# A graph layer on one core: first loads, left-over products, tap transforms and the last gate moved

## Chip, core and metric

The kernel runs on one core of a Trainium2 chip, as one launch. The metric is the device time of that launch in microseconds (us); for several runs it is their median. All data is 32-bit floating point.

In the text PE is TensorE (matrix products), DVE is VectorE, ACT is ScalarE, POOL is GpSimd, and SP is the engine that does nothing but issue transfers. ACT and POOL issue transfers too. An engine works through its own instructions strictly in order.

## What is computed

For 32 graphs (batches) of 512 nodes with 256 channels, with x the input and adj the adjacency matrix:

```python
h = jnp.maximum(_layernorm(x, axis=-1), 0.0)
xc = jnp.transpose(h, (0, 2, 1))
c = relu(_bn(_conv1d(xc, conv1_w, 0), ...))          # 1 tap
c = _bn(_conv1d(c, conv2_w, 8), ...)                 # 17 taps along the nodes
x_conv = jnp.transpose(relu(c + xc), (0, 2, 1))
s = h @ w_se.T + b_se                                # 3 features per node
A = jnp.exp(-dist(s, s)) * adj
x_nmp = einsum('bnm,bmd->bnd', A, relu(h @ w_msg.T + b_msg))
gi = concat([x_conv, x_nmp]) @ w_ih.T + b_ih
gh = h @ w_hh.T + b_hh                               # gates r, z, n of 256 each
r, z = sigmoid(gi_r + gh_r), sigmoid(gi_z + gh_z)
n = tanh(gi_n + r * gh_n)
out = x + (1 - z) * n + z * h
```

## The kernel before, in words

The 17-tap convolution is done in the frequency domain. The nodes of a batch are cut into 8 windows of 64, so that 16 batches fill the 128 partitions; these 16 batches are a *group*, and there are two groups (batches 0 to 15, 16 to 31). A *unit* is one of 40 frequency units of a group: `product` (L368) multiplies the windows' spectra (tile `xf`) with the unit's weights (tile `wt`, two loads of 256 KB from DRAM by `load_unit`, L344), with three complex products. `prepare` (L357) gets for it, on POOL, the sum of the weights (`wsum`, L351) and two combinations of the spectra (`both`, L364 and L365). There are three `wt` buffers, two of `wsum` and two of `both`, so unit u can be loaded when unit u-3 has been used, and prepared when unit u-2 has.

**Stages.** (1) `first_part(0)`, L776: for each batch `statistics` (L279, BNStats and BNStatsAggregate on DVE, a power on POOL), `normalise` (L292, DVE), `transpose_h` (L301, PE transposes, DVE takes the maximum with 0 into `hT`, SP stores it), `conv1` (L311, PE; DVE adds the shift, ACT the relu) and `windows_to_freq` (L326, PE; ACT copies to `xf`). Between these, `weights_to_freq` (L248) turns 64 slices of the tap weights `w2p` into frequency weights. (2) `nodes(0)`, L880: for each batch the messages (`message`, L423), node features (`features`, L438), their distances (`factors`, `affinity`), and `aggregate` (L476); the products of units 0 to 36 are spread over its 16 rounds. (3) `first_part(1)` with the three products that are left over, 37 to 39, given as the lists `left`, of which `fill()` runs one at each of its calls (L800). (4) `nodes(1)` with the 40 products of group two. (5) The late stage: for 16 pairs of batches the inverse transform (`inverse`), and the gates (`gates_rz`, `gate_n`), each as seven products of combined blocks Q1 to Q7. For the last pair the gates r and n come first, and `last_z` (L637) computes z last and the output with it.

**Order.** The two first parts and the late stage stand under `manual_schedule`: each engine gets its instructions in the order of the program text. In the two node loops a scheduling layer orders them. Transfers that one engine issues go out in its order. They signal their end on a few shared counters, and the built program lets an issue wait until the earlier transfer on the same counter has landed; in the profile this is a wait of SP for a transfer that has nothing to do with its own data.

**The places of the change.**
- Start: `first_part(0)` runs the first two steps of `weights_to_freq` ahead of `conv1(0)` (L811 to L817). They need the first slices of `w2p`, which SP loads at L243.
- Group two: x of batches 16 to 18 is loaded by POOL after the node loop (L931); statistics, normalise and the first transposes of batch 16 follow. `left` holds four lists; product 37 comes ahead of the transposes of batch 16, 38 and 39 come after `conv1(16)`.
- End: in `last_z`, the block Q3 (L677) is added in two halves into the bank that held Q5 (`b3`), so it waits until Q5's sum has been read. `blended` (L641) does everything for one quarter in a row: add the other terms (L644), sigmoid on ACT (L647), multiply (L648), transpose 32 by 32 (L652), add to x (L654); `store` (L769) issues four transfers by turns on SP and ACT. `early_out` (L742) writes the n part (transposes L761, add L750); ahead of it `h - n` is computed at L735.

Of the kernel before, what the change touches and what calls it, by code (L numbers as in the profile page):

```python
# [11 lines left out]
FP = mybir.dt.float32  # L12
AF = mybir.ActivationFunctionType
ALU = mybir.AluOpType

P = 128
# [49 lines left out]
def gnn_layer(  # L66
# [38 lines left out]
    def bank(name):  # L105
        return psum.tile([P, N], FP, tag="bank", name=name)
# [7 lines left out]
            queue.dma_start(dst[32 * g : 32 * (g + 1)], src[64 * g : 64 * (g + 1)].rearrange("(e i) o -> i e o", e=DC))  # L114

    def load_x(b, queue=nc.sync):
        X[b] = pools["first"].tile([P, NC, D], FP, tag="x", name=f"x_{b}", bufs=3)
        queue.dma_start(X[b], x[b].rearrange("(c p) d -> p c d", p=P))


# [79 lines left out]
    def shift_w1():  # L200
        nc.scalar.copy(shift1_row.rearrange("p (i q) -> p i q", i=DC), by_parity(row1[1][:, :D]))
# [435 lines left out]
    def last_z(p, terms):  # L637

        d, o, ks = RZ[p], 1, range(K3)

        def blended(src, other, i, j, t=slice(0, N)):  # L641
            z, dst = d[:, DC + i, j, t], d[:, i, j, t]
            if other is not None:
                nc.vector.tensor_add(z, other[:, t], src[:, t])  # L644
                src = z
            g = DC + i
            nc.scalar.activation(z, src, AF.Sigmoid, bias=brz[:, g : g + 1], scale=1.0)  # L647
            nc.vector.tensor_mul(dst, dst, z)  # L648
            js, half = slice(t.start // 32, t.stop // 32), slice(32 * i, 32 * (i + 1))
            if (p, j) not in OUT:  # L650
                OUT[p, j] = pools["late"].tile([P, N // 32, D // 4], FP, tag="o", name=f"o_{p}_{j}", bufs=2)
            nc.vector.transpose(OUT[p, j][:, js, half], dst.rearrange("p (j k) -> p j k", k=32))  # L652
            x = XP[p][j][:, js, half]
            nc.vector.tensor_add(x, x, OUT[p, j][:, js, half])  # L654

        b1, b2, b3, b4 = (bank(f"pz{k}_{p}") for k in range(1, 5))
        into(b1, Q1, o, ks, terms, True)
        p1 = temp("p1", f"z{p}")
        nc.scalar.copy(p1, b1)
        into(b2, Q6, o, ks, terms, True)  # L660
        u2 = temp("u2", f"z{p}")
        nc.vector.tensor_add(u2, p1, b2)
        into(b1, Q2, o, ks, terms, False)
        blended(b1, None, 0, 0)
        early_out(p, 1, 1)
        into(b2, Q7, o, ks, terms, False)
        u3 = temp("u3", f"z{p}")
        nc.vector.tensor_add(u3, p1, b2)
        early_out(p, 0, 1)
        into(b4, Q4, o, ks, terms, True)  # L670
        blended(b4, u3, 1, 0)
        store(p, 0, [nc.sync, nc.scalar])
        into(b3, Q5, o, ks, terms, True)
        blended(b3, u3, 1, 1)
        for h in range(2):
            t = slice(h * N // 2, (h + 1) * N // 2)
            into(b3, Q3, o, ks, terms, False, t)  # L677
            blended(b3, u2, 0, 1, t)
            store(p, 1, [nc.sync, nc.scalar], t)

    def gate_n(p, terms, last):
        rz, o = RZ[p], 2
        NT[p] = nt = pools["late"].tile([P, DC, 2, N], FP, tag="nt", name=f"nt_{p}", bufs=2)
        h, i_ = [0], [1, 2]
        add, mul = ALU.add, ALU.mult

        def pair(q, banks, first):
            for bk, ks in zip(banks, (h, i_)):
                into(bk, q, o, ks, terms, first)

        def scaled(bk, other, other_i, i, j):

            n = nt[:, i, j, :]
            if other is None:
                nc.vector.scalar_tensor_tensor(n, bk, b_hn[:, i : i + 1], rz[:, i, j, :], op0=add, op1=mul)
            else:
                nc.vector.scalar_tensor_tensor(n, bk, b_hn[:, i : i + 1], other, op0=add, op1=add)
                nc.vector.tensor_mul(n, n, rz[:, i, j, :])
                nc.vector.tensor_add(n, n, other_i)

        def closing(bk, i, j):
            n = nt[:, i, j, :]
            nc.vector.tensor_add(n, n, bk)  # L703
            nc.scalar.activation(n, n, AF.Tanh, bias=b_in[:, i : i + 1], scale=1.0)  # L704

        x1 = [bank(f"pn1_{p}_{k}") for k in range(2)]
        pair(Q1, x1, True)
        p1 = [temp("p1", f"n{p}_{k}") for k in range(2)]
        for k in range(2):
            nc.scalar.copy(p1[k], x1[k])  # L710
        x2 = [bank(f"pn2_{p}_{k}") for k in range(2)]
        pair(Q6, x2, True)
        u2 = [temp("u2", f"n{p}_{k}") for k in range(2)]
        for k in range(2):
            nc.vector.tensor_add(u2[k], p1[k], x2[k])
        pair(Q2, x1, False)
        scaled(x1[0], None, None, 0, 0)
        closing(x1[1], 0, 0)
        pair(Q7, x2, False)
        u3 = [temp("u3", f"n{p}_{k}") for k in range(2)]  # L720
        for k in range(2):
            nc.vector.tensor_add(u3[k], p1[k], x2[k])
        x3 = [bank(f"pn3_{p}_{k}") for k in range(2)]
        pair(Q5, x3, True)
        scaled(x3[0], u3[0], u3[1], 1, 1)
        closing(x3[1], 1, 1)
        pair(Q4, x2, False)
        scaled(x2[0], p1[0], p1[1], 1, 0)
        closing(x2[1], 1, 0)
        pair(Q3, x3, False)  # L730
        scaled(x3[0], u2[0], u2[1], 0, 1)
        closing(x3[1], 0, 1)
        for i, j in ((0, 0), (1, 1), (1, 0), (0, 1)):

            nc.vector.tensor_sub(rz[:, i, j, :], HP[p][:, 2 * i + j, :], nt[:, i, j, :])  # L735
            if last and j == 0:
                early_out(p, i, j)
            elif not last:

                blend(p, i, j, nc.gpsimd if p == B // 2 - 2 and i != j else nc.vector)  # L740


    def early_out(p, i, j):
        if (i, j) == (0, 0):
            OUT[p] = pools["work"].tile([P, N // 32, D // 4], FP, tag="x", name=f"on_{p}", bufs=3)
        OUT[p, j] = OUT[p]
        to_tokens(p, j, i)
        o = OUT.pop((p, j))
        if i != j:
            nc.vector.tensor_add(XP[p][j], XP[p][j], o)  # L750

    def blend(p, i, j, engine):
        n, d = NT[p][:, i, j, :], RZ[p][:, i, j, :]
# [25 lines left out]
    def first_part(g, freq, between, left=()):  # L779
# [1 line left out]

        b0, b1 = g * GB, (g + 1) * GB
        for b in range(b0, b0 + 3):
            if b not in X:
                load_x(b)
        if g == 0:
            t = XN[b0] = pools["first"].tile([P, NC, D], FP, tag="xn", name="rows", bufs=2)
# [2 lines left out]
            batch_norm("bn1", scale1, shift1, nc.gpsimd)  # L790
            bn1_row(0, scale1, ones, diags)
            bn1_row(1, shift1, ones, diags)
        statistics(b0)
        normalise(b0)
        if g == 0:
            scale_w1()
            shift_w1()
        left = list(left)

        def fill():  # L800
# [1 line left out]
                step()  # L802

        fill()
        statistics(b0 + 1)
        transpose_h(b0)
        normalise(b0 + 1)
        fill()
        for b in range(b0, b1):
            if b + 3 < b1:  # L810
                load_x(b + 3, nc.gpsimd)  # L811
            if b == b0:
                if g == 0:
                    for steps in between(0):
                        for step in steps:
                            step()
                conv1(b)  # L817
                fill()
            if b + 2 < b1:
                statistics(b + 2)  # L820
            if b + 1 < b1:
                transpose_h(b + 1)
            if b + 2 < b1:
                normalise(b + 2)
            if b == b0:
                fill()
                xf = freq(g)
            one, two = between(b - b0) if b > 0 else ([], [])
            if b > b0:
                conv1(b)  # L830
            if b == b1 - 1:
                load_h(b0)
            for step in one:
                step()
            if b > b0:
                windows_to_freq(b - 1, xf)
            for step in two:
                step()
# [13 lines left out]
    with tc.tile_pool(name="freq", bufs=1) as fpool:  # L852
# [22 lines left out]
                xf = first_part(0, freq_tile, between)  # L875


        LEFT = 3

        def nodes(g, xf, units, last):  # L880

# [32 lines left out]
                for u in mine[2:]:  # L914
                    product(pools["pw"], g, u, xf)

        with phase("pw"):
            with phase("nodes"):
                nodes(0, xf, range(UNITS - LEFT), GB)
            with phase("first", "sums"):  # L920
                combine = combine_weights()

# [5 lines left out]
                    two = [partial(sum_unit, pools["pw"], 1, b - GB + 3)] if b > GB - 3 else []  # L928
                    return combine[b - 2] if 1 < b < len(combine) + 2 else [], two

                for b in range(GB, GB + 3):  # L931
                    load_x(b, nc.gpsimd)

                pw, (u0, u1, u2) = pools["pw"], range(UNITS - LEFT, UNITS)
                left = [[partial(prepare, pw, 0, u1, xf), partial(product, pw, 0, u0, xf)],
                        [partial(prepare, pw, 0, u2, xf)],
                        [partial(product, pw, 0, u1, xf)],
                        [partial(product, pw, 0, u2, xf)]]
                prepare(pw, 0, u0, xf)
                load_unit(0, u1)  # L940
                load_unit(0, u2)
                with tc.manual_schedule():
                    xf = first_part(1, freq_tile, between, left)
            with phase("nodes"):
# [77 lines left out]
```

## Time and profile before

| what | value |
|---|---|
| median of 8 runs | 1866.17 us (1863.29 to 1872.11) |
| the profiled execution | 1870.86 us, of which 1869.1 us span |
| mean granted TensorE clock in it | 0.992 |
| PE busy | 1826.5 us |
| DVE, ACT, POOL busy | 1115.8, 578.2, 580.1 us |
| DMA | 289.25 MB, mean 155 GB/s |

The span goes from the first to the last recorded instruction or transfer; the time of the execution is 1.76 us more. Busy time is time in which an engine has an instruction under way. "Idle before <- releaser" is the time that an engine stood still ahead of an instruction, with what ended it. In a list of waits the numbers are us in total, times, and the longest. In a timeline a row gives the start, the length of a merged run of equal instructions, the engine (SPq, ACTq: issue of transfers), the line, and in brackets the idle time ahead of it. A matmul of 32-bit data shows as two records.

### The profile page before, as it was taken

The page shows a single profiled execution, that of the slowest core. Times are in us where ns is not written, and L with a number is a line of the kernel's source. Part 1 is how long each engine was busy: PE and PEld are TensorE (multiplying, and loading weights), DVE is VectorE, ACT ScalarE, POOL GpSimd, SP SyncE. Part 2 cuts the span into 40 slices and gives each one's busy share as a digit, 9 for nine tenths or more (in the row PEclk, how much of TensorE's full clock was granted, in tenths as well). Part 3 has the DMA queues.
Part 4 walks back from the last instruction along what each step waited for, and adds up shares of the span by engine and source line. Part 5 has one row for each costly group of instructions (what it writes and reads, how often), then busy time and mean ns, then how long its engine had stood idle before and what let it go on. Part 6 is the DMA issues. An engine that isn't in the chain of part 4 may idle for free.

```text
span 1869.1 us, 20076 instructions
## 1 busy us (share of the span) xinstructions
PE 1826.5 (98%) x6598; PEld 1087.7 (58%) x6598; DVE 1115.8 (60%) x2238; ACT 578.2 (31%) x1075; POOL 580.1 (31%) x563
## 2 busy tenths in 40 slices
PE   7999999999899999999999999999999999999997
PEld 5767566666698666666555544555455544555443
DVE  6875555554796554555165566645665466645666
ACT  3455434332145443333222212222122222222121
POOL 3331243344342344442613322132212323133220
PEclk9999999999999999999999999999999999999998
DMA  8998988866567998767513442244422442234412
GB/s 214 297 265 234 214 225 246 218 176 187 186 221 226 228 255 238 228 192 236 179 42 77 119 118 85 37 116 119 112 71 55 118 119 90 52 95 118 118 30 39
DMA packets 306299, 289.25 MB, mean 155 GB/s; under 512 B 148028, under 2 KB 235612, under 8 KB 305812
## 3 DMA queue, kind: packets, MB, share of 16 engines
q1 hardware_dynamic: 279716, 222.64, 45.2%
q10 hardware_dynamic: 19024, 38.68, 5.9%
q0 software_dynamic: 7456, 26.65, 5.2%
q8 instruction: 53, 0.87, 0.2%
q14 instruction: 50, 0.41, 0.1%
HBM read 191.50 MB, written 96.40 MB: 154 GB/s over the span
## 4 chain that ended last, share of the span: by engine, by line
PE 92%; issue 2%; DMA 2%; DVE 2%; POOL 1%; ACT 1%; SPq 0%; ACTq 0%; POOLq 0%; DVEq 0%
PE pg L585 29%; PE pn L585 14%; PE pn L480 11%; PE py L385 10%; PE pc L320 6%; PE pm L431 6%; PE pc L573 5%; PE px L335 4%; PE pw L256 2%; PE pd L466 2%; PE phT L307 1%; PE psr L455 1%; PE pz L585 1%; DMA adj<-in_adj_dram 0%; DMA w_in<-in_w1T_dram 0%
## 5 line engine op out<-in xcount | busy, mean ns | idle before, releaser
L480 PE MATMUL pn<-A,msg 128*128 128x512 f32 x512 | 226.7, 596 | 0.0
L585 PE MATMUL pg<-hp,sw 128*128 128x512 f32 x434 | 221.8, 593 | 0.7 <-DVE rz L604 0.5
L585 PE MATMUL pg<-np,sw 128*128 128x512 f32 x434 | 221.6, 592 | 0.0
L585 PE MATMUL pg<-cp,sw 128*128 128x512 f32 x434 | 221.6, 592 | 0.0
L563 POOL TENSOR_TENSOR hp<-hp 128x512 f32<-128x512 f32 x64 | 80.5, 1269 | 413.3 <-DMA hp<-hd 352.0
L364 POOL TENSOR_TENSOR both<-xf 128x256 f32<-128x256 f32 x78 | 61.0, 782 | 331.1 <-PE py L385 297.2
L480 PEld LDWEIGHTS pn<-A,msg 128*128 128x128 f32 x512 | 97.7, 191 | 111.8 <-issue 108.3
L385 PE MATMUL py<-wt,both 128*128 128x256 f32 x624 | 151.9, 387 | 0.7 <-issue 0.7
L563 POOL TENSOR_TENSOR cp<-cp 128x512 f32<-128x512 f32 x64 | 80.5, 1268 | 226.6 <-ACT cp L579 225.3
L392 DVE TENSOR_TENSOR y<-y,py 128x256 f32<-128x256 f32 x78 | 31.8, 408 | 194.0 <-ACT y L391 194.0
L600 ACT ACTIVATE rz<-rz,brz 128x512 f32<-128x512 f32 x93 | 67.0, 721 | 260.2 <-DVE rz L604 260.2
L585 PEld LDWEIGHTS pg<-hp,sw 128*128 128x128 f32 x434 | 82.2, 190 | 104.8 <-issue 97.3
L585 PEld LDWEIGHTS pg<-cp,sw 128*128 128x128 f32 x434 | 82.5, 190 | 103.8 <-issue 103.6
L585 PEld LDWEIGHTS pg<-np,sw 128*128 128x128 f32 x434 | 82.5, 190 | 103.8 <-issue 103.8
L385 PEld LDWEIGHTS py<-wt,both 128*128 128x128 f32 x624 | 115.1, 192 | 44.2 <-issue 28.3
L472 DVE TENSOR_TENSOR A<-e,at 128x512 f32<-128x512 f32 x128 | 112.1, 914 | 34.9 <-ACT e L469 34.7
L351 POOL TENSOR_TENSOR wsum<-wt 128x512 f32<-128x512 f32 x78 | 108.8, 1396 | 48.6 <-DMA wt<-wd 40.7
L320 PE MATMUL pc<-w,hT 128*128 128x256 f32 x512 | 119.7, 388 | 1.9 <-DVE hT L308 1.9
L431 PE MATMUL pm<-wmsg,hq 128*128 128x259 f32 x512 | 117.8, 382 | 1.8 <-ACT hq L417 1.0
L704 ACT ACTIVATE nt<-nt,vech 128x512 f32<-128x512 f32 x64 | 46.2, 722 | 233.9 <-DVE nt L703 233.9
L585 PE MATMUL pn<-hp,sw 128*128 128x512 f32 x224 | 114.4, 592 | 0.0
L585 PE MATMUL pn<-np,sw 128*128 128x512 f32 x224 | 114.4, 592 | 0.0
(138 smaller groups left out, 2953.3 us busy)
## 6 DMA issues: line engine op xcount, KB each, us to landing
wt<-wd SPq DMA_DIRECT2D x160, 256.0 KB, 4.1
adj<-in_adj_dram SPq DMA_DIRECT2D x128, 256.0 KB, 5.8
wd<-wst SPq DMA_DIRECT2D x64, 320.0 KB, 5.3
yd<-y ACTq DMA_DIRECT2D x80, 256.0 KB, 3.8
yt<-yd SPq DMA_DIRECT2D x30, 640.0 KB, 7.6
hd<-hT SPq DMA_DIRECT2D x32, 512.0 KB, 4.2
nd<-nmp ACTq DMA_DIRECT2D x32, 512.0 KB, 3.6
xb<-in_x_dram SPq DMA_DIRECT2D x128, 128.0 KB, 3.8
```

The lines of the kernel that those rows point to most:

```text
L320: nc.tensor.matmul(p[:, j, :], HT[b][:, ic, c * P : (c + 1) * P], w1[:, ic, :], start=(ic == 0), stop=(ic == DC - 1))
L335: nc.tensor.matmul(p[:, j * 2 * L : (j + 1) * 2 * L], H1[b][:, c0 + j, ic * P : (ic + 1) * P], fwd, start=True, stop=True)
L351: nc.gpsimd.tensor_tensor(t, WT[g, u][:, 0], WT[g, u][:, 1], op=ALU.add)
L364: nc.gpsimd.tensor_tensor(both[:, 0], re, im, op=ALU.add)
L385: nc.tensor.matmul(dst, v[:, ic, :], w[:, ic, :], start=(ic == 0), stop=(ic == DC - 1))
L431: nc.tensor.matmul(p[:, : D + NS], hq[:, ic, c * P : (c + 1) * P], wmsg[:, ic, :], start=(ic == 0), stop=(ic == DC - 1))
L472: nc.vector.tensor_mul(A[b][:, mc, :], e, at)
L480: nc.tensor.matmul(p, MSG[b][:, mc, dc * P : (dc + 1) * P], A[b][:, mc, :], start=(mc == 0), stop=(mc == NC - 1))
L563: nc.gpsimd.tensor_tensor(t[:, dst, :], t[:, a, :], t[:, b, :], op=sub)
L573: nc.tensor.matmul(bk[:, t0:t1], YT[p][j][:, c, oc * P : (oc + 1) * P], back[:, n : n + t1 - t0], start=(c == 0), stop=(c == len(spans) - ...
L585: nc.tensor.matmul(bk[:, t], sw[:, k, q, o, :], terms[k][q][:, t], start=(first and i == 0), stop=(i == len(ks) - 1), skip_group_check=True)
L600: nc.scalar.activation(rz[:, g, j, :], src, AF.Sigmoid, bias=brz[:, g : g + 1], scale=1.0)
```

## The change

1. x of batch 16 gets a buffer of its own, in a new pool "ahead" that is open during the first node loop. It is loaded by SP ahead of that loop's loads, and its statistics are called after the loop; the scheduling layer puts them where it likes. In the built program SP issues the load after the second load of `hT` and ahead of the first `adj`; the four BNStats stand on DVE among the messages of batch 0 (the loop's second), after its second of four, its third, and then its features. x of 17 and 18 is loaded by SP, not POOL, after `normalise(16)`.
2. Four products instead of three are left over (36 to 39). They stand after the transposes of batch 16 (36), after `normalise(17)` (37), after `conv1(16)` (38), and after `normalise(18)` (39). On PE the order after the last `aggregate` was 36, 37, transposes 16, conv1 16, 38, transposes 17, 39, transposes 18; it becomes 35, transposes 16, 36, 37, conv1 16, 38, transposes 17, 39, transposes 18. On SP the loads of units 38 and 39 now stand behind those of x 17 and x 18 and the store of `hT` of batch 16.
3. In first parts the transposes of the first batch come ahead of the statistics of the second, and `conv1` of the first batch ahead of the first two tap transforms.
4. In `last_z` the steps of `blended` are taken apart and interleaved on DVE, Q3 gets two banks of its own, and Q5 is added to `u2`. For the last pair `h - n` (four 128x512) and the n part's add for the pair's second batch (128x1024) go from DVE to POOL.

```diff
 def load_x(b, queue=nc.sync):
-    X[b] = pools["first"].tile([P, NC, D], FP, tag="x", name=f"x_{b}", bufs=3)
+    X[b] = pools["ahead" if b == GB else "first"].tile([P, NC, D], FP, tag="x", name=f"x_{b}", bufs=1 if b == GB else 3)
...
-        def blended(src, other, i, j, t=slice(0, N)):
+        def gated(src, other, i, j, t=slice(0, N)):
...
             nc.scalar.activation(z, src, AF.Sigmoid, bias=brz[:, g : g + 1], scale=1.0)
-            nc.vector.tensor_mul(dst, dst, z)
...
+        def turned(i, j, t=slice(0, N)):
+            dst, (js, half) = d[:, i, j, t], places(i, t)
+            nc.vector.tensor_mul(dst, dst, d[:, DC + i, j, t])
...
             nc.vector.transpose(OUT[p, j][:, js, half], dst.rearrange("p (j k) -> p j k", k=32))
+        def added(i, j, t=slice(0, N)):
...
             nc.vector.tensor_add(x, x, OUT[p, j][:, js, half])
...
         into(b1, Q2, o, ks, terms, False)
-        blended(b1, None, 0, 0)
+        gated(b1, None, 0, 0)
         early_out(p, 1, 1)
+        turned(0, 0)
         into(b2, Q7, o, ks, terms, False)
         nc.vector.tensor_add(u3, p1, b2)
         early_out(p, 0, 1)
+        added(0, 0)
         into(b4, Q4, o, ks, terms, True)
-        blended(b4, u3, 1, 0)
+        gated(b4, u3, 1, 0)
+        into(b3, Q5, o, ks, terms, True)
+        turned(1, 0)
+        gated(b3, u3, 1, 1)
+        nc.vector.tensor_add(u2, u2, b3)
+        added(1, 0)
         store(p, 0, [nc.sync, nc.scalar])
-        into(b3, Q5, o, ks, terms, True)
-        blended(b3, u3, 1, 1)
-        for h in range(2):
-            t = slice(h * N // 2, (h + 1) * N // 2)
-            into(b3, Q3, o, ks, terms, False, t)
-            blended(b3, u2, 0, 1, t)
+        into(b5[0], Q3, o, ks, terms, True, ts[0])
+        gated(b5[0], u2, 0, 1, ts[0])
+        turned(1, 1)
+        into(b5[1], Q3, o, ks, terms, True, ts[1])
+        gated(b5[1], u2, 0, 1, ts[1])
+        added(1, 1)
+        for t in ts:
+            turned(0, 1, t)
+            added(0, 1, t)
             store(p, 1, [nc.sync, nc.scalar], t)
...
-            nc.vector.tensor_sub(rz[:, i, j, :], HP[p][:, 2 * i + j, :], nt[:, i, j, :])
+            (nc.gpsimd if last else nc.vector).tensor_tensor(rz[:, i, j, :], HP[p][:, 2 * i + j, :], nt[:, i, j, :],
+                                                             op=ALU.subtract)
...
-            nc.vector.tensor_add(XP[p][j], XP[p][j], o)
+            (nc.gpsimd if j else nc.vector).tensor_tensor(XP[p][j], XP[p][j], o, op=ALU.add)
...
-            if b not in X:
+            if b not in X and (g == 0 or b == b0):
                 load_x(b)
...
-        statistics(b0)
+        if b0 not in STATS:
+            statistics(b0)
         normalise(b0)
...
+        else:
+            load_x(b0 + 1)
+            load_x(b0 + 2)
...
         fill()
+        transpose_h(b0)
+        fill()
         statistics(b0 + 1)
-        transpose_h(b0)
         normalise(b0 + 1)
         fill()
...
             if b == b0:
+                conv1(b)
                 if g == 0:
                     for steps in between(0):
...
-                conv1(b)
                 fill()
...
-        LEFT = 3
+        LEFT = 4
...
-        with phase("pw"):
+        with phase("pw", "ahead"):
+            load_x(GB)
             with phase("nodes"):
                 nodes(0, xf, range(UNITS - LEFT), GB)
+                statistics(GB)
...
-                for b in range(GB, GB + 3):
-                    load_x(b, nc.gpsimd)
...
-                left = [[partial(prepare, pw, 0, u1, xf), partial(product, pw, 0, u0, xf)],
-                        [partial(prepare, pw, 0, u2, xf)],
-                        [partial(product, pw, 0, u1, xf)],
-                        [partial(product, pw, 0, u2, xf)]]
+                left = [[],
+                        [partial(prepare, pw, 0, u1, xf), partial(product, pw, 0, u0, xf), partial(load_unit, 0, u2)],
+                        [partial(product, pw, 0, u1, xf), partial(load_unit, 0, u3), partial(prepare, pw, 0, u2, xf)],
+                        [partial(prepare, pw, 0, u3, xf), partial(product, pw, 0, u2, xf)],
+                        [partial(product, pw, 0, u3, xf)]]
                 prepare(pw, 0, u0, xf)
                 load_unit(0, u1)
-                load_unit(0, u2)
```

## The prediction

> **What bounds the kernel now.** I read the busy times first, then PE's list of waits, then the timeline at the four changed places.
>
> ```profile
> PE 1826.5 (98%) x6598; PEld 1087.7 (58%) x6598; DVE 1115.8 (60%) x2238; ACT 578.2 (31%) x1075; POOL 580.1 (31%) x563
> ```
>
> PE works 98% of the span, and no product is removed. So the change can only gain or lose PE's standstills, the slow matmuls that follow some of them, and the tail after the last matmul. The waits:
>
> ```profile
> PE phT L307 <- DVE xn L296: 9.0, 5, 3.4
> ...
> PE pz L585 <- DVE rz L644: 3.6, 2, 2.4
> PE psl L450 <- DVE fr L445: 3.0, 3, 1.0
> PE pw L256 <- DMA w2p<-in_w2T_dram: 3.0, 1, 3.0
> PE pd L466 <- DVE y L392: 2.2, 1, 2.2
> PE pc L320 <- DVE hT L308: 1.9, 1, 1.9
> ```
>
> phT, pw and pc wait at the start and at the start of group two, pz at the end, psl and pd at the start of the node loop: all are places that the change rewrites or loads with more.
>
> **Start (first_part(0)).** Now PE waits 3.0 us for w2p until 14.22, does 16 pw records (3.72) and conv1(0) (4.86); DVE's h, then stats, rstd and xn of batch 2 hang on that, and the transposes of batch 2 start at 27.07 after 3.42 us of waiting. Afterwards conv1(0) needs only hT of batch 0. DVE is free for it at 11.84, when w (0.75 from 11.09) is done, and at 484.40 in this trace conv1 starts 0.83 after hT begins: so 12.67, end 17.6. Behind hT (1.28), stats to xn of batch 1 take 4.64 as now (11.76 to 16.40): 17.8; two h 1.4, three pw copies 1.9: stats of batch 2 start at 21.1, now 23.42. That is -2.3; ACT's two relus now stand ahead of its pw copies, and I take **-2.0**, between -2.5 and 0 (0 if transfers pace this stage: their share is 0.93 to 1.00 between 100 and 140 us, but PE waits for none there). A loss would need a later order of something, and nothing else moves.
>
> **Start of the node loop (x of batch 16).** This is the part that costs.
>
> ```profile
> 176.92 0.38 SPq L405 DMA_DIRECT2D hT<-hd  x1
> 177.39 11.71 SPq L401 DMA_DIRECT2D adj<-in_adj_dram  x8
> ...
> 183.50 0.30 PE L450 MATMUL psl<-ident,fl 128*128 128x128 f32 x1 [1.01 <-DVE fr L445]
> ...
> 185.25 1.14 ACT L417 COPY hq<-hT 128x512 f32<-128x512 f32 x2 [6.65 <-DMA hT<-hd]
> ```
>
> The 512 KB of x16 go out between the first two rows, at about 177.4, into the densest transfers of the kernel (share 1.17 from 180 to 190 us): the hT ahead of it, as large, took 8.3 us. DVE reaches the first BNStats at 180.2 and stands there until x16 is in; behind it stand half of batch 0's messages and its features, for which PE's psl waits. If x16 lands L after issue, DVE needs 2.4 more (two BNStats 0.7, two st and msg 1.1, features 0.6), then PE psr 0.6, py 1.9, pm 3.7: batch 1's messages end at 186.0 + L, now at 190.86. With L = 8.6 (the median of hT in this window) that is +3.7. PE stands 6 us for it, and after the 3.42 us at 27.07 slow matmuls cost 2.1 (transposes 2.30 where 1.04 is usual, conv1 4.31 where 3.46 is). Of this 5.8 some is given back: the wait of 2.18 at 230.70, with 2.2 of slow matmuls behind it, comes from transfers of 5.33 and 5.71 us (yd, then hT) that would run in thinner traffic. I take back 2: **+4**. Bounds: L = 4.7 (x on SP in the first 50 us) gives 0, since pm waits for ACT until 187.97 anyway; L = 9.7 (adj, the slowest here) with nothing given back gives +7.
>
> **Start of group two.** Without x16's statistics in the way, PE has work where it now stands:
>
> ```profile
> 473.26 1.89 PE L385 MATMUL py<-wt,both 128*128 128x256 f32 x8
> ...
> 479.44 0.30 PE L307 MATMUL phT<-ident,xn 128*128 128x128 f32 x1 [3.42 <-DVE xn L296]
> ...
> 484.40 5.44 PE L320 MATMUL pc<-w,hT 128*128 128x256 f32 x16 [1.94 <-DVE hT L308]
> ```
>
> One product fewer precedes the last aggregate, so it ends at 468.2, not 470.84. Then five products of 2.6, two sets of transposes of 1.04 and conv1 of 3.46 make 18.5: done at 486.7, now 495.9. So 9.2 are to be had; what is late next? Unit 38's weights. On SP they now stand behind x17, x18 (which waits for the last aggregate) and the store of hT16. hT16 is ready at 473.5. The second half of wt 38 waits, by the shared counters, for the store yd of unit 35 (such waits cost SP 48.3 us in all: "SPq L347 <- DMA yd<-y: 48.3, 14, 7.4"), issued at about 473.0. With this window's medians (yd 2.1, wt 3.1) the weights are in at 478.2, with the page's (3.8, 4.1) at 480.9. POOL, which first does rstd of 17 until 479.0, needs 2.8 for wsum and both (1.26 + 2 x 0.77): product 38 starts at 481.8 to 483.7, where PE is ready at 480.5. I take a wait of 2.2. DVE then does y of 38 ahead of the statistics of 18: from the product's end 0.4 + 0.9 + 1.95 + 1.1 + 0.5 = 4.9 to the transposes of 18, which start at 480.5 + 2.2 + 2.6 + 4.9 = 490.2; now 497.3. That is -7.1; 0.6 for slow matmuls after the wait: **-6.5**. Bounds: -8 with the short wait; +6 if both landings take 9.7 (product 38 at 495.2, 12.5 later, and the 0.6). Behind this, order and work are as before.
>
> On the slow matmuls: after 2.18 us (230.70) and 2.42 us (1856.17) of waiting matmuls ran slow, after 1.42 us (497.3) not. The Trainium skill, "TensorE: Matmul & The Clock Gate", section "HAM oscillation", speaks of gaps above about 3.4 us; by that the wait for product 38 would cost no slow matmuls, and the sum be 0.6 lower.
>
> **End (last_z).**
>
> ```profile
> 1856.17 0.75 PE L585 MATMUL pz<-hp,sw 128*128 128x256 f32 x2 [2.42 <-DVE rz L644]
> ...
> 1859.84 1.22 PE L585 MATMUL pz<-hp,sw 128*128 128x256 f32 x2 [1.21 <-DVE rz L644]
> ...
> 1865.20 0.88 ACTq L772 DMA_DIRECT2D out_dram<-xb  x2
> ```
>
> PE waits 2.42 and 1.21 for the bank of Q3, and runs at half rate after it (0.85 for two records of 256, elsewhere 0.43). With banks of its own Q3 ends at 1853.75 + 2.6 = 1856.4, not 1862.8, and DVE becomes the bound. After Q4 (1851.2): add 0.69, sigmoid 0.72, multiply 0.69, transpose 0.71 with gaps of 0.03: 1854.2; Q5's add, the new u2 + b3 (0.68, as L668) and the add to x: 1856.3; then without pause 0.42 + 0.69 + 0.71 + 0.42 + 0.69 + two times 1.31, and gaps 0.33: last store at 1862.2, now 1865.20: -3.0. The landing behind it stays. POOL's four h - n (1.27 as L563) finish early. Its add of 128x1024 is not in the trace: 1.27 to 2.54, by size the latter. It runs from about 1850.7 to 1853.2, over DVE's multiply at 1852.7. POOL and DVE do hinder each other here:
>
> ```profile
> 1811.47 1.53 DVE L766 TENSOR_TENSOR xb<-xb,o 128x1024 f32<-128x1024 f32 x1
> 1812.00 2.13 POOL L755 TENSOR_TENSOR nt<-nt,rz 128x512 f32<-128x512 f32 x1
> ```
>
> (1.23 and 1.26 alone). I charge 0.5: **-2.5**, between -3.2 and -0.5, the latter if DVE waits for the whole of that add. The rule against this move is in the Trainium skill, "SBUF — State Buffer", section "SBUF: two separate sides": a VectorE operation with two SBUF inputs and a GpSimd one take an exclusive lock, and the second waits for all of the first. By it the end would bring -0.5 at worst, by the rows above, where each lost 0.3 to 0.9, -2 to -3.
>
> **Sum.** -2.0 + 4 - 6.5 - 2.5 = **-7.0**. The profiled execution (1869.1 span, 1.76 around it, 1870.86) would take 1863.9; it is 4.7 over the median of the runs, from which I predict 1866.2 - 7.0 = **1859.2**.
>
> **Rivals.**
> - *x16 lands in time* (L near 4.7, traffic being ahead of compute): the node loop costs 0, sum -11, **1855.2**. For: x on SP took 4.7 early on. Against: hT in the same spot took 8.3.
> - *The stall only moves.* At 477.94 and 484.80 xn took 3.14 where 1.45 is usual, with POOL preparing a unit beside it. If POOL prepares 38 and 39 beside xn of 17 and 18, 3.4 are added, with the long wait of 3.2 and 2 of slow matmuls the boundary gives -0.7, the sum is -1.2: **1865.0**. Against: POOL's rstd, then a wait for weights, leaves xn of 17 mostly alone.
> - *Slower: SP's order.* Loads taken from POOL to SP land late behind each other. With one landing time L at both places (x16; yd 35 and wt 38), the node loop costs L - 4.8 and the boundary 2L - 13.4; with start and end the sum is 3L - 22.7. At L = 9.7 it is +6.4: **1872.6**. It is slower by over 0.2% from L = 8.8. Against: at group two's start transfers run thin (wt 3.1).
>
> **How the numbers follow.** Forecast (-4 to -10) 0.52, x16 in time 0.20, moved stall 0.17, slower 0.11. 0.2% (3.7 us) is about what a measurement of this kernel can tell from no change. Faster by more: 0.52 + 0.20 and a little of the third, 0.74; within: 0.16; slower: 0.10. The range reaches to -13 (first rival with -2 more at the boundary) and to +1: 1853 to 1867.
>
> **What would show it.** Start: no wait of PE for w2p; transposes of batch 2 near 25. Node loop: DVE's stats L284 waiting for DMA x at 178 to 186, psl waiting long. Group two: the 3.42 and 1.94 gone; a wait of py L385 for POOL of 1 to 3. End: no wait of pz for L644; last issue about 9 after Q5's end. I am wrong if that DVE wait is under 2 us (faster), or py waits over 6 (slower).

## The result, and the profile after

The changed kernel takes 1859.96 us (median of 21 runs, 1856.20 to 1865.17) against 1865.48 us before (60 runs): ratio 0.9969, 95% interval 0.9959 to 0.9978, so 4 to 8 us less. The forecast was 1859.2 us. Its profiled execution has a span of 1861.9 us, 7.2 under that of before. That the total fits says little: four terms stand behind it, and some are off in opposite directions.

The busy times and, of PE's waits, the four longest after the first one of all:

```profile
PE 1821.6 (98%) x6598; PEld 1090.0 (59%) x6598; DVE 1107.9 (60%) x2234; ACT 577.7 (31%) x1075; POOL 585.6 (31%) x565
```

```profile
PE psl L450 <- DVE fr L445: 6.1, 3, 4.1
PE phT L307 <- DVE xn L296: 4.9, 2, 3.5
PE pm L431 <- ACT sl L452: 3.7, 1, 3.7
PE py L385 <- POOL both L365: 3.4, 1, 3.4
```

The waits for w2p and for rz L644 are gone, those for xn and hT of batch 16 too, and so is pd's 2.18 at 230.7. Three have come: psl 4.1 at the start of the node loop, py 3.4 at the start of group two (both forecast), and pm 3.7, which was not. Their places in the timeline of the changed kernel, first the node loop:

```profile
174.53 0.38 SPq L405 DMA_DIRECT2D hT<-hd  x1
174.95 0.43 SPq L118 DMA_DIRECT2D x<-in_x_dram  x1
...
182.65 0.43 DVE L284 BATCH_NORM_STATS2 stats<-x 128x6 f32<-128x256 f32 x1 [4.35 <-DMA x<-in_x_dram]
...
184.68 0.45 PE L450 MATMUL psl<-ident,fl 128*128 128x128 f32 x1 [4.08 <-DVE fr L445]
...
185.76 3.62 PE L385 MATMUL py<-wt,xf 128*128 128x256 f32 x8
```

x16 lands 7.7 us after its issue (8.6 assumed). DVE stands 4.35 us at the first BNStats, PE 4.08 at psl, and the product behind it runs at half rate (3.62 where 1.89 is usual; the granted clock is 0.50 from 184 to 190 us). Then the start of group two:

```profile
467.38 1.04 PE L307 MATMUL phT<-ident,xn 128*128 128x128 f32 x8
...
472.81 0.34 SPq L309 DMA_DIRECT2D hd<-hT  x1
...
473.26 2.44 SPq L347 DMA_DIRECT2D wt<-wd  x4
...
477.75 1.27 POOL L351 TENSOR_TENSOR wsum<-wt 128x512 f32<-128x512 f32 x1 [2.53 <-DMA wt<-wd]
...
480.44 3.62 PE L385 MATMUL py<-wt,both 128*128 128x256 f32 x8 [3.39 <-POOL both L365]
...
489.74 1.71 PE L307 MATMUL phT<-ident,xn 128*128 128x128 f32 x8 [1.35 <-DVE xn L296]
```

The transposes of 16 no longer wait, but product 38 does, for weights that SP issues from 473.26 on. SP's list of waits for 460 to 480 us says why so late:

```profile
SPq L309 <- DMA nd<-nmp: 6.9, 1, 6.9
...
SPq L347 <- DMA yd<-y: 0.3, 1, 0.3
```

The store of hT of batch 16 stands ahead of the weights. Its data were ready at 469.9; it waited until 472.8 for the landing of another store, nd of the last aggregate, by a shared counter. The second half of the weights then waited 0.3 us more, for yd of unit 35, which ACT had issued at 469.37 and which landed at 473.96 by the trace; SP sent that half at 473.98. And at the end:

```profile
1846.53 2.72 POOL L770 TENSOR_TENSOR xb<-xb,on 128x1024 f32<-128x1024 f32 x1 [6.03 <-DVE on L781]
...
1850.09 0.60 PE L585 MATMUL pz<-hp,sw 128*128 128x256 f32 x2
...
1852.25 0.59 PE L585 MATMUL pz<-cp,sw 128*128 128x256 f32 x2
...
1856.40 2.12 ACTq L792 DMA_DIRECT2D out_dram<-xb  x4
```

Q3 runs without a wait and at full rate, 1850.09 to 1852.84. The last issue ends at 1858.5; that is 8.3 after Q5's end (1850.25), where before it was 12.3.

Because single waits come and go from one execution to the next, I read every profile by five stretches between fixed points of PE: the first psl (start of the node loop); from there to the fourth aggregate; last aggregate to the transposes of 18; first psl of group two to its last pd; wait of pg for L604 near the end to the end of the span. In us, each from the starts of rows in the timelines; kernels are named as below:

| kernel | loop starts | to agg 4 | boundary | group two's loop | end |
|---|---|---|---|---|---|
| before | 177.17 | 76.74 | 33.51 | 281.19 | 51.71 |
| before_again | 176.99 | 68.74 | 33.95 | 281.21 | 51.74 |
| bound_undone | 174.51 | 70.55 | 33.05 | 281.19 | 48.09 |
| changed | 175.27 | 75.34 | 31.82 | 286.75 | 48.23 |
| after_again | 173.94 | 76.56 | 29.48 | 282.95 | 48.10 |
| start_undone | 176.95 | 75.03 | 33.26 | 282.53 | 48.24 |
| end_undone | 174.50 | 75.29 | 31.64 | 282.45 | 51.72 |
| end_no_pool | 174.68 | 74.86 | 31.50 | 281.22 | 48.46 |
| x16_later | 175.60 | 76.08 | 30.26 | 281.20 | 48.46 |
| x16_later_again | 173.93 | 68.90 | 30.65 | 283.21 | 48.55 |
| stats_later | 172.74 | 75.94 | 29.59 | 283.69 | 48.27 |
| w38_first | 177.82 | 75.95 | 27.69 | 282.13 | 48.13 |
| both_mends | 178.20 | 68.29 | 27.62 | 282.42 | 48.08 |

From the fourth row on, the boundary holds one more product (2.59 us: 209.90 before, 207.31 changed, between the fourth and the last aggregate), which is taken off when they are compared. Between the profiles of before and of the changed kernel the five stretches make 5.5 us of the 7.2; the other 1.7 lie at the last aggregates, which ran slower in the profile of before (15.70 us against 14.00, more at the end).

### The profile page after: what moved, and what is told of

The parts are those of the page before. It is cut to its first block, busy times and chain, and to the rows that moved or that the text cites. A ratio compares the mean times of both kernels' runs of the same rounds, so it can differ in the third digit from the quotient of the medians.

```text
span 1861.9 us, 20075 instructions
## 1 busy us (share of the span) xinstructions
PE 1821.6 (98%) x6598; PEld 1090.0 (59%) x6598; DVE 1107.9 (60%) x2234; ACT 577.7 (31%) x1075; POOL 585.6 (31%) x565
## 4 chain that ended last, share of the span: by engine, by line
PE 91%; DMA 3%; DVE 2%; issue 2%; POOL 1%; SPq 0%; ACT 0%; POOLq 0%; ACTq 0%; DVEq 0%
PE pg L585 29%; PE pn L585 14%; PE pn L480 11%; PE py L385 11%; PE pc L320 6%; PE pm L431 5%; PE pc L573 5%; PE px L335 3%; PE pw L256 2%; PE pd L466 2%; PE phT L307 1%; DMA hT<-hd 1%; PE psr L455 1%; DMA yd<-y 1%; DMA x<-in_x_dram 1%
## 5 line engine op out<-in xcount | busy, mean ns | idle before, releaser
L585 PE MATMUL pn<-cp,sw 128*128 128x512 f32 x224 | 114.4, 592 | 0.0
```

The costliest lines, as they stand in the source:

```text
L585: nc.tensor.matmul(bk[:, t], sw[:, k, q, o, :], terms[k][q][:, t], start=(first and i == 0), stop=(i == len(ks) - 1), skip_group_check=True)
```

## The experiments

Ratios are against runs of the kernel before on the same chip.

**after_again.** No edit.

> The changed kernel once more, beside the variants. Theory: in the first profile two things belong to that one execution and not to the change: the vanished wait at 230.7 us (2.18 us and 2.2 us of slow matmuls behind it in the kernel before) and the wait of PE for hq at 647.8 us (3.73 us, 1.8 us of slow matmuls). Then a second profile has the stall at batch 16's statistics (DVE about 4 us for x, PE about 4 us for psl near 184) again, the wait of 3 to 3.5 us ahead of product 38 again, and no wait of more than 2 us near 647 us; the time is 5 to 6 us under before. Rival: the late hT at 640 us comes from the shifted transfer order of the change; then the wait near 647 us is there again, within 1 us of its size.

Measured: 1860.55 us, ratio 0.9973 (0.9958 to 0.9987). The stall at psl is there again (3.77), the wait ahead of product 38 too (2.68), and no wait over 0.23 us near 230. Near 645 us pm waited 0.91 us, not 3.73. So neither guess holds quite: the place of that wait recurs and its size does not.

**start_undone.** For group one only:

```diff
         fill()
-        transpose_h(b0)
         fill()
         statistics(b0 + 1)
+        transpose_h(b0)
...
-                conv1(b)
                 if g == 0:
                     for steps in between(0):
...
+                conv1(b)
```

> Only group one's start as before, the rest as changed. Theory (the start is worth what the trace shows, 1.9 us, and it is kept to the end because no wait takes it up): 1.5 to 2.5 us slower than the changed kernel, conv1 of batch 1 ends at about 33.4 us instead of 31.6. Rival (the transfers pace the start, so that PE's earlier work waits later): no difference at the start of the node loop, 0 us.

Measured: ratio 0.9987 (0.9973 to 1.0001), 2.6 us more than after_again by the two ratios; that alone is hardly beyond their intervals. conv1 of batch 1 ends at 33.0, and the loop starts at 176.95. With before and before_again that makes a mean of 177.0; the ten profiles with the new start have a mean of 175.1, but lie between 172.7 and 178.2. Clearer is the end of conv1 of batch 1: 33.0 to 33.5 in the three, 29.3 to 31.7 in the ten, 2.6 us less in the mean. So the start is worth 2.6 us where it acts, and 1.9 in the mean at the start of the node loop.

**end_undone.** `last_z`, h - n and the add as in the kernel before (the diff of the change, its fourth part, backwards).

> Only the end as before (last_z, h - n and the n part's add on VectorE), the rest as changed. Theory (the end is worth 3.5 us, as the distance from the end of Q5 to the end of the span shows: 15.35 us before, 11.81 us changed): 3 to 4 us slower than the changed kernel. Rival (my forecast's size): 2.5 us slower. Third (the tail is hidden by the last transfers' landing): under 1 us.

Measured: ratio 0.9987 (0.9973 to 1.0001), again 2.6 us more. The last stretch is 51.72 us, against 48.1 to 48.6 in all ten profiles with the new end: 3.5 us, with almost no scatter. The 3.5 stands.

**end_no_pool.** The new end without GpSimd:

```diff
-            (nc.gpsimd if last else nc.vector).tensor_tensor(rz[:, i, j, :], HP[p][:, 2 * i + j, :], nt[:, i, j, :],
-                                                             op=ALU.subtract)
+            nc.vector.tensor_sub(rz[:, i, j, :], HP[p][:, 2 * i + j, :], nt[:, i, j, :])
...
-            (nc.gpsimd if j else nc.vector).tensor_tensor(XP[p][j], XP[p][j], o, op=ALU.add)
+            nc.vector.tensor_add(XP[p][j], XP[p][j], o)
```

> The changed kernel with h - n and the n part's last add back on VectorE, the interleaving and the two banks of Q3 kept. The forecast charged GpSimd's add 0.5 us; the changed trace shows no such loss. Theory (GpSimd's share is a gain: VectorE has four of 0.69 and one of 1.23 us more ahead of Q4's add, and is 0.7 us idle there): from the first matmul of Q3 to the end of the span 12.3 to 13.8 us, now 11.7 to 11.8, so 0.5 to 2 us slower. Rival (VectorE has room, or GpSimd hinders it): 11.2 to 11.9 us, no difference.

Measured: ratio 0.9951 (0.9937 to 0.9965), last stretch 48.46 us. From the first matmul of Q3 to the end of the span it takes 12.2 us, against 11.8 in the changed kernel and 11.6 to 12.1 in the nine profiles with GpSimd's share. That lies between the two ranges: what goes to GpSimd gains 0.1 to 0.6 us, by the profile that is compared. Where it comes from shows in the add behind Q4, first here, then in the changed kernel:

```profile
1842.79 0.68 DVE L644 TENSOR_TENSOR rz<-u_z,pz 128x512 f32<-128x512 f32 x1
```

```profile
1847.72 0.69 DVE L644 TENSOR_TENSOR rz<-u_z,pz 128x512 f32<-128x512 f32 x1 [0.69 <-PE pz L585]
```

Here DVE comes to it without a pause, 2.0 us ahead of Q5's end; in the changed kernel DVE has stood idle for 0.69 us and starts it 2.5 us ahead. The gain of the end is thus nearly all of Q3's two banks and the interleaving; the two were not tried apart. This kernel's ratio is 4 us under that of after_again, with intervals that overlap. Its one profile has no loss in group two's loop (281.22), which isn't of its edit; whether that holds for its other runs was not seen.

**x16_later** and **x16_later_again.** x16 loaded in the ninth round:

```diff
         with phase("pw", "ahead"):
-            load_x(GB)
             with phase("nodes"):
...
+                if g == 0 and i == 8:
+                    load_x(GB)
                 aggregate(b)
```

> x of batch 16 is loaded in the ninth round of the node loop instead of ahead of its first, and its statistics stand behind product 14; all else as changed. Theory A (the stall at the start of the node loop is paid in the time): DVE no longer waits for x there, PE's psl waits 1.0 us and not 4.1, and the kernel is 3.5 to 4.5 us faster than the changed one, about 10 us under before. Theory B (it is given back at once, since the transfers that made PE wait 2.18 us at 230.7 us in the kernel before run in thinner traffic): that wait comes back and the time stays within 1.5 us of the changed kernel.

> The later x16 once more. Its first profile took as long from the start of the node loop to the fourth aggregate as the changed kernel (76.1 us against 75.3), with a wait of 1.43 us for y at 226.9 us and slow matmuls, though its time was 6 us lower in the median. Theory A (paid: the wait for y is a chance of single executions): this profile has no such wait, 70 to 72 us for that stretch, and the median is again 4 to 6 us under the changed kernel. Theory B (given back): the wait is there again, 75 to 77 us, and the gain in the time comes from another stretch; then the wait of PE for sl near 645 us, 0.5 to 3.7 us in all four profiles with x16 early and absent here, is the candidate, worth 1.3 us and up.

Measured: ratios 0.9942 (0.9923 to 0.9961) and 0.9945 (0.9926 to 0.9963), some 5 to 6 us under after_again. Both times psl waits 1.0 us or less. To the fourth aggregate the first took 76.08 us and the second 68.90: PE's wait for y is in one and not in the other. In the first:

```profile
226.94 2.53 PE L466 MATMUL pd<-sr,sl 9*128 9x512 f32 x4 [1.43 <-DVE y L392]
```

So Theory A holds for the time, and the wait for y is there in some executions and not in others.

**stats_later.** The early load stays, and the statistics are tied to the ninth round:

```diff
+                if g == 0 and i == 8:
+                    t = X[GB][:, :, 0:1]
+                    nc.vector.scalar_tensor_tensor(t, MSG[b][:, :, 0:1], 0.0, t, op0=ALU.mult, op1=ALU.add)
                 aggregate(b)
```

> As the changed kernel, x of 16 loaded at the same early place on SP, but its statistics tied to the ninth round by one extra VectorE operation of 128x4 (x plus zero times a message, which leaves x as it is). Theory (the cost lies in VectorE standing in its order at the BNStats, not in the transfer): psl waits 1.0 us and not 4, the stretch from the start of the node loop to the fourth aggregate is 69 to 71 us when no chance wait falls into it, and the time is that of the later load, 4 to 6 us under the changed kernel. Rival (the 512 KB in front of adj cost as much by delaying adj and hT): messages of batch 1 still end 3 to 4 us late, and the time is within 1.5 us of the changed kernel.

Measured: ratio 0.9937 (0.9913 to 0.9962), in which one run of 10 ms is left out; that is some 7 us under after_again. The stall is gone with the load where it was:

```profile
178.74 0.30 PE L450 MATMUL psl<-ident,fl 128*128 128x128 f32 x1 [0.67 <-DVE fr L445]
```

The first aggregate starts 16.11 us into the loop, against 21.0 to 21.8 with the statistics early. With the load itself later it starts 15.0 and 15.8 us into the loop, so the transfer costs some 1 us at most (0.3 and 1.2 against the two); nearly all of the stall was DVE standing in its order at the BNStats. The stretch to the fourth aggregate is 75.94 all the same: the wait for y (1.04 at 223.9) fell into this profile.

**before_again.** No edit.

> The kernel before once more, for its waits. In its first profile PE waited 2.18 us for y at 230.7 us; the kernel with group two's order of before had no such wait, a kernel with the later x16 had 1.43 us at that place in one of two profiles. If it is a chance of single executions: no wait over 1 us near 230 us here, 70 to 71 us from the start of the node loop to the fourth aggregate. If it belongs to this order: the wait again, about 76 us. Near 645 us no wait of PE in either case, if that one comes with the new order of group two.

Measured: 1864.13 us in its one run, no wait of PE near 230 us or 645 us, 68.74 us to the fourth aggregate. The wait of 2.18 that the profile of before showed is not in every execution of that kernel.

**bound_undone.** Group two's start and x16 as in the kernel before, `LEFT = 3`, start and end as changed.

> Group two's start and the load of x16 as before, the start and the end as changed. By the stretches of the traces the start is worth 1.9 us and the end 3.5 us. Theory (what the new order at group two's start gains, 1.7 to 4 us, is about what x16 costs in the node loop): within 1.5 us of the changed kernel, 5 to 6 us under before. Rival (the new order is worth its gain and the stall is given back): 3 to 4.5 us slower than the changed kernel, 1 to 2 us under before.

Measured: 1859.65 us, ratio 0.9970 (0.9958 to 0.9982), the same as the changed kernel. What the new order at group two gains, x16 in the node loop and the loss in group two's loop take away again. This sets the two largest terms of the forecast against each other without any profile.

**w38_first.** Unit 38's weights ahead of x17 and x18 on SP, and its preparation ahead of rstd of 17 on POOL:

```diff
-                        [partial(prepare, pw, 0, u1, xf), partial(product, pw, 0, u0, xf), partial(load_unit, 0, u2)],
-                        [partial(product, pw, 0, u1, xf), partial(load_unit, 0, u3), partial(prepare, pw, 0, u2, xf)],
+                        [partial(prepare, pw, 0, u1, xf), partial(product, pw, 0, u0, xf), partial(prepare, pw, 0, u2, xf)],
+                        [partial(product, pw, 0, u1, xf), partial(load_unit, 0, u3)],
...
                 load_unit(0, u1)
+                load_unit(0, u2)
```

> The changed kernel with one edit: the weights of unit 38 are loaded ahead of x of 17 and 18 and of the store of hT of batch 16, and POOL prepares unit 38 behind product 36's preparation of 37 and ahead of rstd of 17. Theory (product 38 waits because its weights stand third on SP's queue, so that POOL gets them at 477.7 us): PE's wait ahead of product 38, 2.7 to 3.8 us in the profiles of the changed kernel and its variants, is gone or under 0.5 us, the transposes of 18 come 4 to 5.5 us earlier, the kernel is 3 to 5 us faster than the changed one. Rival (x of 17 takes the place of the weights): statistics of 17 wait for x, the transposes of 17 wait 3 us or more, and the time is within 1.5 us of the changed kernel.

Measured: 1857.58 us, ratio 0.9952 (0.9935 to 0.9969), about 4 us under after_again; the two intervals overlap, so the gain rests on the profile as well.

```profile
469.91 0.90 SPq L347 DMA_DIRECT2D wt<-wd  x2
...
480.05 1.89 PE L385 MATMUL py<-wt,both 128*128 128x256 f32 x8
...
484.67 1.99 PE L385 MATMUL py<-wt,both 128*128 128x256 f32 x8 [1.00 <-POOL both L365]
```

The weights go out at 469.91 with nothing ahead of them, and product 38 (480.05) follows conv1 without a wait. What is left is 1.00 ahead of product 39. The boundary takes 27.69 us against a mean of 31.0 in the eight profiles with the changed kernel's order: 3.3 us, where 4 to 5.5 were expected.

**both_mends.** x16_later and w38_first together.

> x of 16 loaded in the ninth round, and the weights of unit 38 ahead of x of 17 and 18: both edits on top of the changed kernel. If both act where they stand: as far under the kernel with only the later x16 as the earlier weights are worth alone, 3 to 5 us, so some 14 to 15 us under before (about 1852 us). If the second only moves a wait of the other: the same as the later x16 alone.

Measured: 1851.85 us (1848.85 to 1854.27), ratio 0.9921 (0.9904 to 0.9938), some 15 us under before by the ratio. Both act where they stand. This version beats both kernels.

## Why the prediction was right, and where it was not

*Start, -2.0.* The mechanism was right: PE no longer waits for w2p, and the transposes of batch 2 start at 24.30 (near 25 forecast). The gain is 2.6 at the end of conv1 of batch 1, just over the bound of 2.5. The 1.9 at the start of the node loop is so near to the forecast in part by luck. The profiles of w38_first and both_mends lose 3.6 and 4.0 us in between: PE waits 1.9 and 1.8 us near 90 us, where it waits 1.0 to 1.4 in all others, and slow matmuls follow. Their edits don't touch this stretch; why the wait is longer there was not tried. The end of conv1(0) at 17.75 (17.6 forecast) is luck too: it started 0.7 earlier than forecast and ran slow (5.74 us for 4.86). In the nine other profiles with the new start it ended at 14.9 to 16.3.

*Start of the node loop, +4.* Right in size, wrong in how. Six profiles with the early statistics take 74.9 to 76.6 us to the fourth aggregate, mean 75.5; the three with before's order 68.7, 70.6 and 76.7, mean 72.0: +3.5. The mechanism was as forecast, and stats_later shows it. What failed is "I take back 2". The wait at 230.7 was read from one profile as if it were part of the kernel. It costs 5 to 7 us when it occurs (40.1 to 41.7 from the second to the fourth aggregate, 34.7 to 35.3 without it), in 3 of the 7 profiles without the stall and in none of the 6 with it; these are too few to tell whether the stall keeps it away. The four profiles with neither take 68.3 to 70.6 us, mean 69.1, so the stall by itself costs 6.4, where the forecast had 5.8 ahead of the 2. Against the profile of before the stall was given back in full (-1.4 over this stretch), against the other two hardly at all. That +3.5 is near +4 in the mean is thus in part luck. The three medians with the stall removed (x16_later twice, stats_later) are 5 to 7 us under after_again, with intervals of 3 to 5 us either way.

*Start of group two, -6.5.* The sign was right and the size too large: 33.5 (mean of three) plus the product of 2.59 less 31.0 is 5.1, and 4.3 between the first two profiles. The term that was mis-sized is the wait ahead of product 38, with the slow matmuls behind it. PE is ready for it as forecast (480.5 in before's time is 477.2 here; it was 477.05), and what makes the weights late is what was named: their second half waits for yd of unit 35. That store went out when it was forecast, 2 us after the transposes of 16 began, but it took 2.9 to 4.6 us to land in the eight profiles, mean 3.6, and the second half another 2.9 to 4.8, mean 4.2. The forecast had 2.1 and 3.1 as the short case, 3.8 and 4.1 as the long one, and took a wait in the middle, 2.2. The runs came out at the long one: the wait was 2.2 to 3.8 us, mean 3.1, and slow matmuls behind it cost between nothing and 2.8 (in start_undone its two rows took 3.78 and 1.91, where 1.89 and 1.03 are usual); 0.6 was charged. That the store of hT was held by nd, up to 472.8 and not 470.2 as forecast, was not foreseen, but it did little: in four of the eight profiles the second half went out only on yd's landing, in the other four 0.1 to 0.3 us after it.

*"Behind this, order and work are as before."* The work is, the times are not. Group two's loop took 281.2 us in all three profiles with before's order there; in the ten with the new order it took 0 to 5.6 more, 1.7 in the mean. In the changed kernel's first profile:

```profile
626.69 13.30 SPq L347 DMA_DIRECT2D wt<-wd  x4
...
630.78 0.62 ACT L417 COPY hq<-hT 128x512 f32<-128x512 f32 x1 [7.99 <-DMA hT<-hd]
630.84 0.33 ACTq L394 DMA_DIRECT2D yd<-y  x1
...
640.08 0.38 SPq L405 DMA_DIRECT2D hT<-hd  x1
...
646.70 0.62 ACT L417 COPY hq<-hT 128x512 f32<-128x512 f32 x1 [7.28 <-DMA hT<-hd]
```

As I read these rows, it is a ring of queues. ACT's copy waits for hT; the store yd stands behind the copy; SP's next weights wait for that store (two waits for yd, 15.7 us together, between 615 and 650 us); the next hT stands behind the weights; and PE's messages wait for it, 3.73 us at 647.8. The loss goes with how late that next hT is issued: 5.9 to 7.1 us after the second aggregate's start there is none (five profiles, before's order and new), at 7.4 to 8.5 it is 0.9 to 2.5 us (seven), at 10.5, in the profile shown, 5.6. How late the first hT is does not tell: SP issues it 5.3 us ahead of the second aggregate in before_again, which loses nothing, and 6.9 us ahead in end_undone, which loses 1.3. Why the new order of group two makes the next hT later in eight of its ten profiles wasn't tried.

*End, -2.5.* The mechanism was right and the gain 3.5, outside the bounds of -3.2 to -0.5. Two terms were mis-sized. GpSimd's add was charged 0.5 and cost 0.1: it took 2.72 us, and DVE's multiply starts 0.01 us after its end and 0.10 after the sigmoid (1849.16) for which it waits anyway (0.46 after it in the two profiles of x16_later). And the DVE chain from Q3's first half to the last add took 5.2 us (1852.39 to 1857.59), 0.7 less than the sum of its parts with gaps: an operation that doesn't need the result of the one before it starts 0.07 to 0.09 us ahead of that one's end, and a gap of 0.03 or 0.04 stands only ahead of one that does. The Trainium skill, "SBUF — State Buffer", section "SBUF: two separate sides", lets a VectorE operation with two SBUF inputs and a GpSimd one that reads SBUF exclude each other, the second waiting for all of the first. The changed kernel's trace agrees, a little earlier:

```profile
1839.24 1.26 POOL L754 TENSOR_TENSOR rz<-hp,nt 128x512 f32<-128x512 f32 x1 [2.17 <-ACT nt L723]
...
1839.66 1.93 DVE L770 TENSOR_TENSOR xb<-xb,on 128x1024 f32<-128x1024 f32 x1
```

GpSimd's subtraction ends at 1840.50, and the add beside it, begun before that, 1.09 later; it takes 0.70 us more than without GpSimd (1.23 at 1841.05 in end_no_pool). So it is luck of the timing that the last add on GpSimd cost so little: it ended just when the multiply was due.

*The sum.* -1.9 + 3.5 - 5.1 + 1.7 - 3.5 = -5.3, measured 4 to 8 less. Of the rivals, "x16 lands in time" falls (7.7 us). "The stall only moves" falls in its mechanism: xn of 17 and 18 took 1.38 and 1.45, not 3.14; the loss of 1.7 in group two's loop is one that no rival named. "SP's order" is right in its place but small: it costs 3.3 us, by w38_first, where the rival had product 38 come 12.5 us later.

## What to carry to other kernels

A wait that one profile shows may be a chance of that execution: before a term is built on it, look for it in a second profile of the same order of work. Where work is hoisted into another stage, ask first what stands behind it on its engine: here a load cost some 1 us at most and the four instructions that read it cost PE's standstill. And on a queue that issues transfers in order, put the load that the next product needs ahead of the stores, since an issue may wait for a landing that has nothing to do with it.

## What the runs showed of the hardware

How long PE stood still does not decide alone whether the matmuls after it are slow. Product 38 in x16_later and in x16_later_again:

```profile
481.59 2.00 PE L385 MATMUL py<-wt,both 128*128 128x256 f32 x8 [3.46 <-POOL both L365]
```

```profile
471.42 3.67 PE L385 MATMUL py<-wt,both 128*128 128x256 f32 x8 [2.15 <-POOL both L365]
```

After 3.46 us of waiting it runs at its usual rate (2.00), after 2.15 us at half of it (3.67). The granted clock is 1.00 from 481 to 485 us in the first, and 0.57 from 471 to 475 us in the second. The Trainium skill, "TensorE: Matmul & The Clock Gate", section "HAM oscillation", puts the bound at gaps of some 3.4 us; here slow and usual rates lie on both sides of it.

The traces' records of the granted clock show what decides at this place. In each of the 13 traces all the times at which that clock changes lie whole multiples of 3.413 us apart, to within 0.003. So every execution is divided into equal stretches, and they lie differently in each. In x16_later_again the 2.15 us fall into one stretch, 468.17 to 471.58, and the clock is at half for the next one, to 474.99. In x16_later the 3.46 us are split at 479.71, into 1.58 and 1.88, and the clock stays at 1.00. The other six profiles go the same way: with 2.4 to 3.3 us of the wait in one stretch product 38 is slow (the changed kernel, start_undone, end_undone, end_no_pool), with 1.7 at the most it is not (after_again, stats_later).

At other places less is enough, and idle time is not all that counts. The last aggregates, behind a wait of 1.11 us in both, in the changed kernel and in after_again:

```profile
881.74 14.00 PE L480 MATMUL pn<-A,msg 128*128 128x512 f32 x32
```

```profile
877.18 15.70 PE L480 MATMUL pn<-A,msg 128*128 128x512 f32 x32
```

In after_again the wait lies in one stretch, in the changed kernel across two. But it lies in one stretch in six other profiles too, and their aggregates are not slow; what else counts there was not tried. For a forecast it means that such a wait has a cost behind it, 0 to 2.8 us at product 38, which the length of the wait alone does not give.
